# Edge lists on 128 partitions of 416 columns in a four-layer graph network

## The chip, the cores and the metric

The program runs on one core of a Trainium2 chip. The metric is device time in microseconds of one execution. A core has a matrix engine (PE, with its weight loads shown as PEld), a vector engine (DVE, VectorE), a scalar engine (ACT), a general engine (POOL, GpSimd) and a queue engine (SP, SyncE), each of which works through its own list of instructions in order. Data come and go by DMA. In this kernel SP and ACT issue plain transfers, and POOL issues the indirect ones: a gather reads one table row per partition by an index, and a scatter writes one.

## What is computed

The graph has 3125 nodes of 256 features and 53125 directed edges, sorted by destination (`dst`). Every edge has a source (`src`), 64 features (`edge_attr`) and one of 64 types. Four layers follow each other, each on the layer-normed, rectified nodes and each added to them:

```python
h = relu(layernorm(x)); x = x + L0(h)   # messages by an MLP, summed over dst; node MLP; layer norm
h = relu(layernorm(x)); x = x + L1(h)   # attention with a term by edge type, softmax over dst
h = relu(layernorm(x)); x = x + L2(h)   # attention with a term by edge features, softmax over ALL edges
h = relu(layernorm(x)); x = x + L3(h)   # graph attention, softmax over dst, then one LSTM step
```

L2 differs from the others: it takes the softmax over all edges, swaps the two ends of the edge, and therefore wants the edges by their source.

```python
dst, src = edge_index[0], edge_index[1]        # L2 is called with edge_index = (src, dst)
alpha = softmax((q[dst] * (k[src] + edge_attr @ We)).sum(-1) / sqrt(32), axis=0)
out = segment_sum(v[src] * alpha, dst)
```

## The kernel before

**Prelude** (`prelude`, L243). It sorts the nodes by degree and builds all lists. The edge lists are laid out as 125 partitions of 425 columns (`EP, EC`), which holds exactly 53125 edges. `dst_i` is loaded on SP's queue (L254), `e_src`, `e_typ` and `nxt_i`, the destination of the next edge, on ACT's (L261 to L267). `counted` (L325) counts edges per node: VectorE writes one comparison per value (`ol`, `oh`, L330 and L332) over a half of the columns, and PE adds up one outer product per column (L334). `table` (L353) makes the first layer's source rows, which SP stores (L366). The nodes are scattered in sorted order, and for every node the list of its edges' sources and types is gathered from `s_src_type` (`st`).

For L2 every edge gets a place in a table by source, `s_src_records` (`ss`): 440 tiles of 128 rows of 66 numbers (64 features, destination, source within its block of 128 nodes), 18 tiles for each block of 128 source nodes and 8 for the last. VectorE ranks the edges within their block (comparisons L456, running sums L463, then L519 to L555), which ends in the row number `row2`. More rows exist than edges; the whole table is filled beforehand with zeros and a source of -1 by 40 transfers from `sfill` (L305).

**Layers** (`by_slots`, L560). L0 works on 226 pairs of slots. For each, POOL gathers two tiles of source rows (`gt`, L154), PE multiplies edge features (L924), and VectorE adds and sums (L938, L943). L1 goes by blocks of 128 nodes in groups of four slots: per group SP loads the types (`tb`, L980), POOL gathers up to four tiles (`kv`), VectorE forms the scores (L992 to L996), and PE sums the weighted values (L1032). A ring of ten `kv` buffers lies between POOL and these sums. L2 reads `s_src_records` in tiles (`srec`, L1188) and L3 gathers again (`xg`).

**The records are scattered during L0 and L1.** `scatter_src` (L597) scatters one column of edges per call, 425 calls: one per pair from the 19th on, one per step while L0's last work drains, and the rest spread over L1's groups. Columns come in chunks of `CH = 5`: `loaded` (L585) has SP load the features of a chunk into one of two `rec` buffers (L588), and `filled` (L591) has VectorE copy the destination and source into them (L592, L593). Both must wait until the chunk two back has been scattered out of that buffer.

**Order.** Instructions are written in the order of the Python code, and a scheduler places them in each engine's list ahead of what they do not depend on. POOL's gathers and scatters are tied in a written order: `Kit.queued` (L139) sets each scatter after the gather before it and each gather after the last of either kind. An engine waits in order: a load on SP that waits for its buffer holds every transfer behind it.

Of the kernel before, what the change touches and what calls it, by code (L numbers as in the profile page):

```python
# [50 lines left out]
assert sum(TILES) == NT  # L51
XH = 516
# [171 lines left out]
class Lists:  # L224


    def __init__(self, pool):
        self.nid_i = pool.tile([P, NB], I32, name="nid_i")
        self.nid3_i = pool.tile([P, NB], I32, name="nid3_i")
        self.off_i = pool.tile([P, NB], I32, name="off_i")  # L230
        self.deg = pool.tile([P, NB], F32, name="deg")
        self.has = pool.tile([P, NB], F32, name="has")
        self.st = pool.tile([P, NB, SM, 2], I32, name="st")
        self.pen = pool.tile([P, NB, SM], F32, name="pen")
        self.srcb = pool.tile([P, NB, 2, HM], I32, name="srcb")
        self.ai = pool.tile([P, 2, NB], I32, name="ai")
        self.row2 = pool.tile([EP, EC], I32, name="row2")
        self.dst_e = pool.tile([EP, EC], F32, name="dst_e")
        self.srcl_e = pool.tile([EP, EC], F32, name="srcl_e")
# [3 lines left out]
def prelude(ctx, tc, a, a_d, nodes_d, ss, st_d, flag, t):  # L243
# [9 lines left out]
    dst_i = c.tile([EP, EC], I32, name="dst_i")  # L253
    nc.sync.dma_start(dst_i, a["dst"].rearrange("(p c) -> p c", c=EC))  # L254
# [5 lines left out]
    e_src = c.tile([EP, EC], I32, name="e_src")  # L260
    nc.scalar.dma_start(e_src, a["src"].rearrange("(p c) -> p c", c=EC))  # L261
    e_typ = c.tile([EP, EC], I32, name="e_typ")
    nc.scalar.dma_start(e_typ, a["edge_type_64"].rearrange("(p c) -> p c", c=EC))
    nxt_i = c.tile([EP, EC], I32, name="nxt_i")
    nc.gpsimd.memset(nxt_i, N)
    for p0, p1, w in ((0, EP - 1, EC), (EP - 1, EP, EC - 1)):
        nc.scalar.dma_start(nxt_i[p0:p1, 0:w],  # L267
                            bass.AP(tensor=a["dst"].tensor, offset=a["dst"].offset + p0 * EC + 1,
                                    ap=[[EC, p1 - p0], [1, w]]))
# [6 lines left out]
    sfill = c.tile([P, 11, SREC], F32, name="sfill")  # L276
# [12 lines left out]
    nc.gpsimd.memset(cap[:, NB - 1:NB], float(P * TILES[NB - 1]))  # L289
    none = c.tile([1, 512], F32, name="none")  # L290
# [13 lines left out]
    for i in range(40):  # L304
        nc.sync.dma_start(ss[i * 11 * P:(i + 1) * 11 * P, :].rearrange("(p r) c -> p (r c)", p=P),  # L305
                          sfill.rearrange("p r c -> p (r c)"))

    both_e = c.tile([EP, EC, 2], I32, name="both_e")
    nc.gpsimd.tensor_copy(both_e[:, :, 0], e_src)
    nc.gpsimd.tensor_copy(both_e[:, :, 1], e_typ)  # L310
    nc.scalar.dma_start(st_d.rearrange("(p c) -> p c", c=2 * EC), both_e.rearrange("p c i -> p (c i)"))


    lo_i = wk.tile([EP, EC], I32, name="lo_i", tag="edge", bufs=4)
    nc.vector.tensor_scalar(lo_i, dst_i, 127, None, op0=ALU.bitwise_and)
    lo = c.tile([EP, EC], BF, name="lo")
    nc.vector.tensor_copy(lo, lo_i)
    hi_i = wk.tile([EP, EC], I32, name="hi_i", tag="edge", bufs=4)
    nc.vector.tensor_scalar(hi_i, dst_i, 7, None, op0=ALU.logical_shift_right)
    hi = c.tile([EP, EC], BF, name="hi")  # L320
    nc.vector.tensor_copy(hi, hi_i)
    pdeg = ps.tile([P, NB], F32, name="pdeg")
    CW = 214

    def counted(hp, c0, c1):  # L325
        w = c1 - c0
        ol = hp.tile([EP, P, CW], BF, name="ol")
        oh = hp.tile([EP, NB, CW], BF, name="oh")
        for v in range(P):
            nc.vector.tensor_scalar(ol[:, v, 0:w], lo[:, c0:c1], float(v), None, op0=ALU.is_equal)  # L330
        for v in range(NB):
            nc.vector.tensor_scalar(oh[:, v, 0:w], hi[:, c0:c1], float(v), None, op0=ALU.is_equal)  # L332
        for i in range(w):
            nc.tensor.matmul(pdeg, ol[:, :, i], oh[:, :, i], start=(c0 + i == 0), stop=(c0 + i == EC - 1))  # L334
# [33 lines left out]
    with tc.tile_pool(name="ph", bufs=1) as hp:  # L368
        counted(hp, 0, CW)
        stats()  # L370
        table(0, 5)
        counted(hp, CW, EC)
# [73 lines left out]
    sl_i = wk.tile([EP, EC], I32, name="sl_i", tag="edge", bufs=4)  # L446
    nc.vector.tensor_scalar(sl_i, e_src, 127, None, op0=ALU.bitwise_and)
    nc.vector.tensor_copy(t.srcl_e, sl_i)
    hs_i = wk.tile([EP, EC], I32, name="hs_i", tag="edge", bufs=4)
    nc.vector.tensor_scalar(hs_i, e_src, 7, None, op0=ALU.logical_shift_right)  # L450
    hs = c.tile([EP, EC], BF, name="hs")
    nc.vector.tensor_copy(hs, hs_i)
    eq = op.tile([EP, NB, EC], BF, name="eq")
# [3 lines left out]
    zero = ps.tile([EP, EC], F32, name="zero")  # L457
    nc.vector.memset(zero, 0.0)
    cum = op.tile([EP, NB, EC], F32, name="cum")
# [8 lines left out]
    tots = c.tile([EP, NB], F32, name="tots")  # L468
    nc.vector.tensor_copy(tots, cum[:, :, EC - 1])
    pc3 = ps.tile([P, 4, NB], F32, name="pc3")  # L470
    pc2, pv = pc3[:, 0:2, :], pc3[0:1, 2, :]
    nc.tensor.matmul(pc2[:EP, 0, :], k.tri[:EP, :EP], tots, start=True, stop=True)
    nc.tensor.matmul(pc2[:, 1, :], k.ones[:EP, :], tots, start=True, stop=True)
    viol = wk.tile([EP, EC], F32, name="viol", tag="edge", bufs=4)
    nc.vector.tensor_tensor(viol, dst_i, nxt_i, ALU.is_gt)
    v1 = c.tile([EP, 1], F32, name="v1")
# [5 lines left out]
    nc.vector.tensor_tensor(over, pc2[:, 1, :], cap, ALU.is_gt)  # L482
    v3 = c.tile([P, 1], F32, name="v3")
    nc.vector.tensor_reduce(v3, over, AX.X, ALU.add)
    nc.tensor.matmul(pv[:, 0:1], v1, k.ones[:EP, 0:1], start=True, stop=False)
# [5 lines left out]
    bases = c.tile([EP, NB], F32, name="bases")  # L491
    nc.vector.tensor_scalar(bases, pc2[:EP, 0, :], -1.0, None, op0=ALU.add)
# [4 lines left out]
    for b in range(NB - 1, -1, -1):  # L497
        k.gather(t.st[:, b, 0:SLOTS[b], :].rearrange("p s i -> p (s i)"), flat(st_d, 2 * E), t.off_i[:, b:b + 1], axis=1)
# [46 lines left out]
    pos_i = wk.tile([EP, EC], I32, name="pos_i", tag="edge", bufs=4)  # L545
    nc.vector.tensor_copy(pos_i, cum[:, 0])
    pa_i = wk.tile([EP, EC], I32, name="pa_i", tag="edge", bufs=4)
    nc.vector.tensor_scalar(pa_i, pos_i, 127, None, op0=ALU.bitwise_and)
    pj_i = wk.tile([EP, EC], I32, name="pj_i", tag="edge", bufs=4)
    nc.vector.tensor_scalar(pj_i, pos_i, 7, None, op0=ALU.logical_shift_right)  # L550
    step = wk.tile([EP, EC], F32, name="step", tag="edge", bufs=4)
# [3 lines left out]
    nc.vector.scalar_tensor_tensor(t.row2, hs, float(P * TM), step, op0=ALU.mult, op1=ALU.add)  # L555
    nc.vector.tensor_scalar(t.dst_e, dst_i, float(KVQ), None, op0=ALU.mult)
# [3 lines left out]
def by_slots(ctx, tc, a, out, a_d, nodes_d, ss, t):  # L560
# [19 lines left out]
    attr = a["edge_attr_64"].rearrange("(p c) k -> p c k", c=EC)  # L580
    CH = 5
    recs = ctx.enter_context(tc.tile_pool(name="s_recs", bufs=2))
    done = [0]

    def loaded(c):  # L585

        rec = recs.tile([EP, CH, SREC], F32, name="rec")
        nc.sync.dma_start(rec[:, :, 0:64], attr[:, c:c + CH, :])  # L588
        return rec

    def filled(c, rec):  # L591
        nc.vector.tensor_copy(rec[:, :, 64], dst_e[:, c:c + CH])  # L592
        nc.vector.tensor_copy(rec[:, :, 65], srcl_e[:, c:c + CH])  # L593

    rec_of = {}

    def scatter_src(n):  # L597

        for _ in range(n):
            c = done[0]  # L600
            if c == EC:
                return
            c0 = c - c % CH
            if c == 0:
                rec_of[0] = loaded(0)
                filled(0, rec_of[0])
            if c % CH == 1 and c0 + CH < EC:
                rec_of[c0 + CH] = loaded(c0 + CH)
            if c % CH == 3 and c0 + CH < EC:
                filled(c0 + CH, rec_of[c0 + CH])  # L610
            k.scatter(ss, row2[:, c:c + 1], rec_of[c0][:, c % CH, :], "src_records")
# [341 lines left out]
    with tc.tile_pool(name="s_e1", bufs=2) as wk, tc.tile_pool(name="s_e1w", bufs=1) as w, \  # L953
# [159 lines left out]
        left, shares, share = EC - 8 - done[0], sum(-(-c // U) for c in SLOTS), 0  # L1113
# [16 lines left out]
        scatter_src(EC)  # L1130
# [1206 lines left out]
def kernel(tc: tile.TileContext, a: dict, out: bass.AP):  # L2337
# [3 lines left out]
    ss = nc.dram_tensor("s_src_records", [NT * P, SREC], F32, kind="Internal").ap()  # L2341
    st_d = nc.dram_tensor("s_src_type", [2 * E], I32, kind="Internal").ap()
# [43 lines left out]
```

## Time and profile before

| what | before |
|---|---|
| median of 4 runs | 3778.4 us (3776.03 to 3781.05) |
| the profiled execution's own time | 3780.2 us |
| its span | 3778.1 us |
| busy: PE, DVE, ACT, POOL | 2353.4, 2378.4, 1096.8, 2483.7 us |
| mean granted TensorE clock | 0.773 of full |
| moved by DMA | 595.89 MB, mean 158 GB/s |

The span is the time from the first instruction to the last in one profiled execution. The stages can be told apart in the trace: the prelude ends at about 240 us, L0's pairs run from there to 1257 us, what is left of L0 drains until 1387, L1 runs to 2317, L2 to about 3095, and L3 to the end. A line of a group gives the source line, engine, operation, names of output and inputs with their shapes and the count; then busy time and mean nanoseconds of one; then how long the engine stood idle just before, and what ended most of that. Busy time leaves out the short gap between two instructions of an engine. A wait is named by its releaser; "issue" means that nothing in the profile was waited for.

### The profile page before, as it was taken

What the parts mean: (1) busy time and instruction counts of PE and PEld (TensorE: products, weight loads), DVE (VectorE), ACT (ScalarE), POOL (GpSimd) and SP (SyncE); (2) the same over time, 40 slices, a digit from 0 to 9 for tenths busy, and PEclk for the clock granted to TensorE, in tenths of its full rate; (3) what the DMA queues carried; (4) which work ended last, traced back from release to release, by engine and by line L of the source; (5) the groups of instructions that cost most, each with busy time, mean ns of one, the idle gap of its engine ahead of it and who ended that gap; (6) DMA issues with size and microseconds to landing.
All of it is one profiled execution on the core that took longest, in us unless ns stands there. A gap on an engine that the chain in (4) does not pass through costs nothing. (4 is left out here: it accounts for less than half of the span.)

```text
span 3778.1 us, 32562 instructions
## 1 busy us (share of the span) xinstructions
PE 2353.4 (62%) x9174; PEld 1477.7 (39%) x9174; DVE 2378.4 (63%) x4836; ACT 1096.8 (29%) x2296; POOL 2483.7 (66%) x2497
## 2 busy tenths in 40 slices
PE   5818778788877654556656665898989950112223
PEld 3404434344343334445544543566666640001111
DVE  5547566566666426667767765788888953444444
ACT  1112222222221112122322221566666630112222
POOL 3447677777777736767767654666666617667774
PEclk9858989998898765666767767899999975555556
DMA  6336565666666345656666554666666623333342
GB/s 225 128 112 177 138 182 163 171 173 171 183 169 173 84 134 164 173 162 191 188 172 193 170 156 157 204 196 206 198 209 200 192 92 107 100 97 105 108 112 72
DMA packets 295839, 595.89 MB, mean 158 GB/s; under 512 B 113501, under 2 KB 154508, under 8 KB 295650
## 3 DMA queue, kind: packets, MB, share of 16 engines
q0 software_dynamic: 163616, 472.86, 43.2%
q1 hardware_dynamic: 131512, 119.79, 10.6%
q8 instruction: 76, 1.25, 0.1%
q10 hardware_dynamic: 522, 1.06, 0.1%
q14 instruction: 113, 0.93, 0.1%
HBM read 510.85 MB, written 82.21 MB: 157 GB/s over the span
## 5 line engine op out<-in xcount | busy, mean ns | idle before, releaser
L154 POOL DMA_INDIRECT kv<-s_l_rows,dst x440 | 456.1, 1037 | 218.8 <-issue 74.6
L158 POOL DMA_INDIRECT s_src_records<-rec,row x425 | 512.7, 1206 | 131.4 <-issue 121.2
L924 PE MATMUL ph<-wm,st 128*128 128x512 f32 x904 | 473.7, 652 | 131.1 <-DVE acc L943 64.7
L154 POOL DMA_INDIRECT gt<-s_l_src,srcb x452 | 433.8, 960 | 175.9 <-issue 106.1
L154 POOL DMA_INDIRECT kv<-s_l_kv,st x439 | 420.1, 957 | 182.9 <-issue 112.9
L154 POOL DMA_INDIRECT xg<-s_l_rows,src x439 | 416.5, 949 | 133.7 <-issue 133.4
L990 PE MATMUL pk<-rel,toh 64*128 64x64 f32 x878 | 181.8, 368 | 307.8 <-DVE mk L992 180.9
L938 DVE TENSOR_TENSOR ph<-gt,ph 128x1024 f32<-128x1024 f32 x226 | 276.7, 1225 | 109.7 <-PE ph L924 98.3
L134 PE MATMUL pt<-ident,hb 128*128 128x128 f32 x50 | 16.9, 441 | 511.3 <-ACT hb L1436 511.3
L924 PEld LDWEIGHTS ph<-wm,st 128*128 128x128 f32 x904 | 177.7, 207 | 334.4 <-issue 292.8
L990 PEld LDWEIGHTS pk<-rel,toh 64*128 64x128 f32 x878 | 162.5, 272 | 340.9 <-issue 241.2
L1032 PE MATMUL acc<-kv,ident 128*128 128x256 f32 x878 | 246.9, 450 | 40.1 <-DVE kv L1028 40.1
L1287 PE MATMUL pg<-kv,oh 128*128 128x256 f32 x880 | 253.5, 414 | 3.7 <-DVE kv L1284 3.4
L592 DVE COPY rec<-dst_e 125x5 f32<-125x5 f32 x85 | 16.6, 196 | 378.7 <-DMA s_src_records<-rec,row 338.6
L985 ACT ACTIVATE toh<-tb,negp 64x512 f32<-64x512 f32 (+3 forms) x119 | 81.8, 688 | 577.8 <-PE pk L990 510.3
L943 DVE SCALAR_TENSOR_TENSOR acc<-ph,acc 128x1024 f32<-128x1024 f32 x201 | 244.7, 1217 | 3.0
L1032 PEld LDWEIGHTS acc<-kv,ident 128*128 128x128 f32 x878 | 200.1, 231 | 79.9 <-DVE kv L1028 43.5
L1472 DVE TENSOR_SCALAR sc<-xg,own 128x4 f32<-128x4 f32 (+3 forms) x119 | 29.6, 248 | 311.4 <-DMA xg<-s_l_rows,src 311.3
L134 PEld LDWEIGHTS pt<-ident,hb 128*128 128x128 f32 x50 | 7.2, 201 | 540.8 <-ACT hb L1436 540.1
L1429 DVE SCALAR_TENSOR_TENSOR acc<-xg,sc,acc 128x256 f32<-128x256 f32 x439 | 210.5, 487 | 5.2
L1242 PE MATMUL pk<-we,eat 64*128 64x256 f32 x880 | 162.1, 442 | 47.3 <-DVE mk L1248 46.1
L1248 DVE TENSOR_TENSOR mk<-kv,pk 128x512 f32<-128x512 f32 x220 | 149.2, 678 | 48.6 <-DMA kv<-s_l_rows,dst 41.3
(373 smaller groups left out, 5386.7 us busy)
## 6 DMA issues: line engine op xcount, KB each, us to landing
s_src_records<-sfill SPq DMA_DIRECT2D x40, 363.0 KB
srec<-s_src_records SPq DMA_DIRECT2D x24, 594.0 KB
rec<-in_edge_attr_dram SPq DMA_DIRECT2D x85, 156.2 KB
tb<-s_slot_types SPq DMA_DIRECT2D x101, 128.0 KB
gt<-s_l_src,srcb POOLq DMA_INDIRECT x452, 3.6
kv<-s_l_rows,dst POOLq DMA_INDIRECT x440, 3.8
kv<-s_l_kv,st POOLq DMA_INDIRECT x439, 3.9
xg<-s_l_rows,src POOLq DMA_INDIRECT x439, 2.8
```

Of the source, the lines that this page charges most:

```text
L154: self.queued(lambda: self.nc.gpsimd.indirect_dma_start(out=to, out_offset=None, in_=table, in_offset=bass.IndirectOffsetOnAxis(ap=index, ...
L158: st = self.queued(lambda: self.nc.gpsimd.indirect_dma_start(out=table, out_offset=bass.IndirectOffsetOnAxis(ap=index, axis=0), in_=rows, ...
L924: nc.tensor.matmul(ph[:, h, :], stat[h][:, s % 4, :], ms[b][h], start=True, stop=True)
L938: nc.vector.tensor_add(ph, gt, ph)
L943: nc.vector.scalar_tensor_tensor(accs[b], ph, 0.0, accs[b], op0=ALU.max, op1=ALU.add)
L985: nc.scalar.activation(to, tb[:, 0:n * P], AF.Abs, bias=negp[:64])
L990: nc.tensor.matmul(pk[:, q, :], toh[:, q, :], rel, start=True, stop=True)
L1032: nc.tensor.matmul(acc, ident, v[:, q, :], start=(s0 + q == 0), stop=(s0 + q == C - 1))
L1242: nc.tensor.matmul(pk[:, i, :], eat[i * 64:(i + 1) * 64, q, :], we[i * 64:(i + 1) * 64, :], start=True, stop=True)
L1248: nc.vector.tensor_add(mk, o.kv[j // 2][:, :, 0:D], pk)
L1287: nc.tensor.matmul(pg, oh[:, j % T6 + i, :], v[:, i, :], start=(j + i == 0), stop=(j + i == n - 1))
L1429: nc.vector.scalar_tensor_tensor(acc, xgs[q // U3][:, q % U3, 0:D], s[:, q:q + 1], acc, op0=ALU.mult, op1=ALU.add)
```

## The change

The edge lists are laid out on all 128 partitions in 416 columns (`ECW`). Partition 127 then holds 293 edges (`EL`) and 123 places without one. Such a place gets source and destination 4096 and type 0, by transfers of its own from a row of constants, and its record goes to rows that are added behind the table (`past`). Each of the four loads of the prelude is thus made of a part of 127 partitions and small parts for the last one.

The fill of `s_src_records` covers only the last three rows that a partition has in each block (`FULL` counts those that are sure to be overwritten, and a new check, `low`, sends any input with too few edges in a block to the kernel's other path).

The chunk becomes four columns, in a ring of three buffers that are cleared once. The features of a chunk are asked for two chunks ahead instead of one; the copies stay one chunk ahead. A chunk in columns past 293 loads 127 partitions.

All other operations on the edge lists keep their form, with 128 partitions and 416 columns in place of 125 and 425.

```diff
-    dst_i = c.tile([EP, EC], I32, name="dst_i")
-    nc.sync.dma_start(dst_i, a["dst"].rearrange("(p c) -> p c", c=EC))
+    none_i = c.tile([1, 3, ECW], I32, name="none_i")
+    for i, v in enumerate((32 * P, 0, 64 * P)):
+        nc.gpsimd.memset(none_i[:, i, :], v)
+
+    def edges(engine, to, of, i):
+        engine.dma_start(to[0:P - 1, :], of[0:(P - 1) * ECW].rearrange("(p c) -> p c", c=ECW))
+        engine.dma_start(to[P - 1:P, 0:EL], of[(P - 1) * ECW:E].rearrange("(p c) -> p c", p=1))
+        engine.dma_start(to[P - 1:P, EL:ECW], none_i[:, i, EL:ECW])
+
+    dst_i = c.tile([P, ECW], I32, name="dst_i")
+    edges(nc.sync, dst_i, a["dst"], 0)
...
-    e_src = c.tile([EP, EC], I32, name="e_src")
-    nc.scalar.dma_start(e_src, a["src"].rearrange("(p c) -> p c", c=EC))
+    e_src = c.tile([P, ECW], I32, name="e_src")
+    edges(nc.scalar, e_src, a["src"], 0)
...
-    for p0, p1, w in ((0, EP - 1, EC), (EP - 1, EP, EC - 1)):
+    nc.scalar.dma_start(nxt_i[P - 1:P, EL - 1:ECW], none_i[:, 2, EL - 1:ECW])
+    for p0, p1, w in ((0, P - 1, ECW), (P - 1, P, EL - 1)):
...
+    past = c.tile([1, ECW - EL], I32, name="past")
+    nc.gpsimd.iota(past, pattern=[[1, ECW - EL]], base=NT * P, channel_multiplier=0)
+    sfill = c.tile([P, 3, SREC], F32, name="sfill")
...
-    for i in range(40):
-        nc.sync.dma_start(ss[i * 11 * P:(i + 1) * 11 * P, :].rearrange("(p r) c -> p (r c)", p=P),
-                          sfill.rearrange("p r c -> p (r c)"))
+    for b0, b1_ in ((0, 12), (12, NB - 1), (NB - 1, NB)):
+        n = TILES[b0]
+        r0 = b0 * P * TM
+        nc.sync.dma_start(ss[r0:r0 + (b1_ - b0) * P * n, :].rearrange("(b p j) c -> p b (j c)", p=P, j=n)
+                          [:, :, FULL[b0] * SREC:n * SREC],
+                          sfill.rearrange("p r c -> p (r c)")[:, None, :].to_broadcast([P, b1_ - b0, 3 * SREC]))
...
+    nc.vector.tensor_tensor(low, low, pc2[:, 1, :], ALU.is_gt)
+    nc.vector.tensor_add(over, over, low)
...
     nc.vector.scalar_tensor_tensor(t.row2, hs, float(P * TM), step, op0=ALU.mult, op1=ALU.add)
+    nc.sync.dma_start(t.row2[P - 1:P, EL:ECW], past)
...
-    CH = 5
-    recs = ctx.enter_context(tc.tile_pool(name="s_recs", bufs=2))
+    attr = a["edge_attr_64"]
+    CH = 4
+    recs = ctx.enter_context(tc.tile_pool(name="s_recs", bufs=1))
+    ring_ = [recs.tile([P, CH, SREC], F32, name=f"rec{i}") for i in range(3)]
+    for rec in ring_:
+        nc.gpsimd.memset(rec, 0.0)
...
-        rec = recs.tile([EP, CH, SREC], F32, name="rec")
-        nc.sync.dma_start(rec[:, :, 0:64], attr[:, c:c + CH, :])
-        return rec
+        rec = ring_[c // CH % 3]
+        full = min(CH, max(0, EL - c))
+        for p, w0, w1 in ((P, 0, full), (P - 1, full, CH)):
+            if w1 > w0:
+                nc.sync.dma_start(rec[0:p, w0:w1, 0:64],
+                                  bass.AP(tensor=attr.tensor, offset=attr.offset + (c + w0) * 64,
+                                          ap=[[ECW * 64, p], [64, w1 - w0], [1, 64]]))
...
             if c == 0:
-                rec_of[0] = loaded(0)
-                filled(0, rec_of[0])
-            if c % CH == 1 and c0 + CH < EC:
-                rec_of[c0 + CH] = loaded(c0 + CH)
-            if c % CH == 3 and c0 + CH < EC:
-                filled(c0 + CH, rec_of[c0 + CH])
-            k.scatter(ss, row2[:, c:c + 1], rec_of[c0][:, c % CH, :], "src_records")
+                loaded(0)
+                filled(0)
+                loaded(CH)
+            if c % CH == 1 and c0 + 2 * CH < ECW:
+                loaded(c0 + 2 * CH)
+            if c % CH == 3 and c0 + CH < ECW:
+                filled(c0 + CH)
+            k.scatter(ss, row2[:, c:c + 1], ring_[c // CH % 3][:, c % CH, :], "src_records")
```

## The prediction

> **What bounds the kernel now.** I read the page first, for the engines and the costliest groups; then the busy time by stretch, cut where the stages change; then the timeline of POOL; then the waits, and the DMA queues in narrow windows.
>
> ```profile
> PE 2353.4 (62%) x9174; PEld 1477.7 (39%) x9174; DVE 2378.4 (63%) x4836; ACT 1096.8 (29%) x2296; POOL 2483.7 (66%) x2497
> L158 POOL DMA_INDIRECT s_src_records<-rec,row x425 | 512.7, 1206 | 131.4 <-issue 121.2
> L592 DVE COPY rec<-dst_e 125x5 f32<-125x5 f32 x85 | 16.6, 196 | 378.7 <-DMA s_src_records<-rec,row 338.6
> ```
>
> No engine is near full over the span. The scatter of edge records is POOL's costliest group, and VectorE stands idle 338.6 us before the record copies. Both are averages, so I cut the span: L0's pairs (320 to 1257 us), L0's tail, and L1 (1387 to 2317).
>
> ```profile
> core 0: us, PE busy (x) PEld busy (x) DVE busy (x) ACT busy (x) POOL busy (x), PEclk, DMA share, GB/s
> 320.00:1257.00 937.00, 755.10 (x2196) 378.77 (x2195) 590.37 (x850) 197.09 (x401) 708.61 (x682) 0.90 0.59 168
> 1257.00:1337.00 80.00, 41.40 (x94) 21.88 (x92) 23.71 (x66) 7.15 (x15) 63.69 (x54) 0.71 0.28 66
> 1387.00:2317.00 930.00, 542.47 (x2106) 426.68 (x2106) 639.17 (x1035) 217.83 (x357) 639.10 (x624) 0.68 0.62 176
> ```
>
> The same stretches, the scatter of records alone:
>
> ```profile
> 320.00:1257.00 937.00, 252.08 (x208) 0.90 0.59 168
> 1257.00:1337.00 80.00, 61.72 (x52) 0.71 0.28 66
> 1387.00:2317.00 930.00, 198.90 (x165) 0.68 0.62 176
> ```
>
> POOL's timeline shows what its busy figure leaves out, 0.30 us between any two instructions:
>
> ```profile
> 1327.28 0.98 POOL L158 DMA_INDIRECT s_l_kv<-kv,nid_i  x1 [0.30 <-issue]
> 1328.57 1.19 POOL L158 DMA_INDIRECT s_src_records<-rec,row  x1 [0.30 <-issue]
> 1330.06 1.18 POOL L158 DMA_INDIRECT s_src_records<-rec,row  x1 [0.30 <-issue]
> ```
>
> With it POOL is occupied 708.6 + 682 x 0.30 = 913 of 937 us in L0 (97%), all of the tail, and 639.1 + 624 x 0.30 = 826 of 930 us in L1 (89%). POOL bounds L0 and nearly L1, so VectorE's wait at the record copies is mostly VectorE being early.
>
> **The change, part by part.** The profiled execution took 3780.2 us (span 3778.1), 1.8 above the median of 3778.4; I sum against 3780.2 and take 1.8 off at the end.
>
> *The scatter's price.* 425 scatters of 125 rows become 416 of 128. Whatever their row length, the trace's 128-row scatters are cheaper (min/median/max ns):
>
> ```profile
> L158 POOL DMA_INDIRECT s_src_records<-rec,row x425: 1172/1210/1499, 320.3 to 2306.8; - x142
> L158 POOL DMA_INDIRECT s_l_kv<-kv,nid_i x25: 958/998/1011, 505.5 to 1383.5; - x25
> L158 POOL DMA_INDIRECT s_nodes<-xh,rank_i x25: 956/960/4620, 133.7 to 167.7; - x25
> ```
>
> In the timeline above both kinds stand side by side, 0.98 against 1.18. No 128-row scatter of 264-byte rows is in the trace: bounds 0.96 and 1.21. I take 0.98, because the neighbouring rows are nearest in all but row length.
> - L0's pairs: 208 x (1.212 - 0.98) = 48.3; at 97%, **-47**. PE is next: 755 of 890 us, 85%.
> - Tail: 52 x (1.187 - 0.98) = **-11**. Then come 50 us of PE, ACT and VectorE chain with POOL waiting for kv, left as they are.
> - L1: the schedule puts 260 scatters ahead of L1 in both programs, so the nine dropped ones are L1's: 9 x 1.505 = 13.5. The other 156 x (1.205 - 0.98) = 35.1. At 89% of 48.6, **-43**.
>
> *The record loads.* 85 loads of 125 x 5 become 104 chunks of 128 x 4, in a ring of three instead of two. A load waits for the same scatter as before but is needed eight scatters later, not five; a copy waits for a scatter eight back. What a late copy would hold is VectorE's queue, and in L0 POOL is the bound, so I cost this at 0 there; with that cover gone it could give part of the waits named in rival 1. From column 293 on partition 127 holds no edge: 31 loads, all in L1, and one of three columns take 127 partitions. In the tail, one load of now:
>
> ```profile
> DMA packets 692, 0.21 MB, mean 76 GB/s; under 512 B 678, under 2 KB 678, under 8 KB 692
> q1 hardware_dynamic: 617, 0.16, 25.5%
> ```
>
> This window is 1262.05 to 1264.75: 617 of a load's 625 packets of 256 bytes took 0.255 x 16 x 2.7 = 11.0 us of engine time in 2.7 us, 17.9 ns each, so about five engines at once. 125 is 5 x 25; 127 has no divisor, so I take all 508 packets on one engine: 508 x 17.9 = 9.1 us, stretched by the gathers' 0.62 share of it to 9.1 / 0.38 = 24 us at worst. A chunk of four scatters now lasts 930 / 165 x 4 = 22.5 us in L1, and a load has eight scatters of lead, so it should land in time. The transfers for slot types queue behind it on SP, but in the trace they are issued 30 us or more before their use nearly throughout. What is left is the gathers' share on that engine:
>
> ```profile
> DVE mk L992 <- DMA kv<-s_l_kv,st: 53.1, 21, 5.8
> POOL kv L154 <- PE acc L1032: 53.5, 23, 13.8
> ```
>
> I let the first wait grow by a fifth, **+10**; bounds 0 (127 spreads as 125 does) and +112 (rival 2).
>
> *The start.* dst, src, type and next-dst now load 127 partitions each; 25 rows per engine become 127 on one by the same reasoning.
>
> ```profile
> DVE lo_i L315 <- DMA dst_i<-in_dst_dram: 6.7, 1, 6.7
> PE pa L361 <- DMA b<-in_L_gnn_eb_dram: 25.6, 1, 25.6
> q10 hardware_dynamic: 392, 0.64, 7.7%
> ```
>
> The last line is ACT's queue over the first 30 us: 0.077 x 480 / 392 = 94 ns for a packet of some 1.7 KB. dst alone: (127 - 25) x 94 ns = +9.6 us; taking turns with ACT's three loads, +19. VectorE starts later by that, and x and bias b, queued behind dst on SP, hold the first count. Bounds +10 and +22; I take **+16**, since the loads do start together. The small pieces for the last partition, among them the padding behind POOL's three new memsets, are inside the bounds.
>
> *Edits that I cost at little.* The fill shrinks from 40 transfers of 363 KB to three, 2.5 MB in all. SP was through with them at 72 us, when the first row block (70.5 + 0.6) was ready, and from 66.6 to 100.7 PE is busy 34.07 of 34.1 us, which hides it: 0; without that cover the ready row block gains 1 us. PE has 9 count matmuls fewer, 0.7 us. The 2% narrower counts, scans and sums on VectorE give 53 us x 9 / 425 = 1.1. Against these, SP waits for row2 (239.3 us) to patch the padding rows before it reads the flag and loads L0's weights, where it went on at 237.6: with the issue, some 2.5. Three memsets of the ring (0.31 each, by xh's) stand ahead of POOL's first gather: 1. The check's two VectorE instructions (0.2 each) lie beside POOL's slot gathers: 0. Together **+2**.
>
> Sum: -47 - 11 - 43 + 10 + 16 + 2 = -73; 3780.2 - 73 - 1.8 = **3705**.
>
> *The skill against this change.* The trace's row is the load above, about five engines at 125 partitions. The Trainium skill, page "DMA: Bandwidth & Descriptors", section "Why a DMA increments its semaphore by 16 and not by 1", says that a transfer runs on the largest number of engines, at most 16, that divides the slowest dimension of both its sides: 5 for 125, 16 for 128, one for 127. By that rule the loads at the start and in late L1 get slower while the scatters spread; it would give the sum above. By the measured five engines kept for 127, the two terms would go: 3679.
>
> **The rivals.**
> 1. *The deeper ring frees VectorE as well.* For: in L1 POOL waits 53.5 us for PE's acc, which follows VectorE, and VectorE waits 107.8 us there for the scatters. Against: the fills keep POOL's pace in any ring. If 40 of those go and the load term is 0: 3705 - 40 - 10 = 3655.
> 2. *The one-engine loads become L1's bound; slower.* The engine does 0.62 x 22.5 = 14.0 us per chunk besides; it decides once a load costs it over 22.5 - 14.0 = 8.5 us, and with 17.9 ns it costs 9.1. For: that is the edge. Against: the share counts packets waiting for memory. At 24 ns, 12.2 us: 3.6 us x 31 chunks = +112 in place of -43 + 10: 3705 + 33 + 112 = 3850.
> 3. *The same, only to the edge:* L1 gains nothing: 3705 + 33 = 3738, up to 3760 with a slow start.
> 4. *The scatter's price belongs to its short rows* and stays 1.21: only nine calls go, -12: 3778.4 - 12 + 28 = 3794. Against: the 0.98 beside 1.18 above.
>
> **How the numbers follow.** My case 0.58 (its own range 3680 to 3740); rival 1 0.16; rival 3 0.13; rival 2 0.07; rival 4 0.06. A measurement here tells about 0.2%, 7.6 us. Faster: my case, rival 1 and nearly all of rival 3, 0.85; same 0.03; slower, rivals 2 and 4, 0.12. The range leaves out rivals 2 and 4 and a part of rival 1: 3645 to 3775.
>
> **What would show it.** Right: records scatters near 0.98 us; L0's pairs about 47 us shorter; the first VectorE compare after 18 us; L1 30 to 45 us shorter. Wrong: scatters at 1.2 us; POOL waiting for rec's load in L1; gathers landing far later than their median of 3.9 us.

## The result and the profile after

| | before | after |
|---|---|---|
| median | 3777.1 us (62 runs, 3762.4 to 3792.2) | 3787.9 us (38 runs, 3773.9 to 3797.5) |
| after over before | | 1.0027, 95% interval 1.0021 to 1.0033 |
| span of the profiled execution | 3778.1 us | 3786.6 us |

The change makes the kernel slower, by 0.27%. I had forecast 3705 us, 1.9% faster. Since a total can hide gains and losses that meet, the first step is to cut both spans at the same events. Each boundary is the start of a POOL instruction in the trace (us):

| stage | before | after | step | predicted |
|---|---|---|---|---|
| start of the span to the first gather of L0 (`gt`) | 245.7 | 276.6 | +30.9 | +18 (start and handover) |
| to the first record scatter | 74.6 | 74.2 | -0.4 | 0 |
| L0's pairs, to the last `gt` gather | 934.1 | 895.3 | -38.8 | -47 |
| L0's tail, to the first `kv` gather of L1 | 132.9 | 127.6 | -5.3 | -11 |
| L1, to the last scatter of L2's rows | 953.6 | 966.3 | +12.7 | -33 (-43 and +10) |
| L2 and L3 | 1437.2 | 1446.5 | +9.3 | 0 |

The scatters did what was forecast. The page of the kernel after (busy time, mean ns of one, idle before):

```profile
PE 2341.0 (62%) x9165; PEld 1472.2 (39%) x9165; DVE 2375.2 (63%) x4876; ACT 1097.1 (29%) x2296; POOL 2388.7 (63%) x2496
...
L162 POOL DMA_INDIRECT s_src_records<-rec,row x416 | 416.3, 1001 | 128.7 <-issue 118.2
```

A record scatter takes 1001 ns instead of 1206, and POOL is busy 95 us less in the whole program. By stretch (L0's pairs, its tail, L1), the kernel after:

```profile
core 0: us, PE busy (x) PEld busy (x) DVE busy (x) ACT busy (x) POOL busy (x), PEclk, DMA share, GB/s
350.80:1246.10 895.30, 746.94 (x2195) 376.71 (x2194) 590.47 (x870) 197.97 (x401) 667.99 (x681) 0.91 0.61 175
1246.10:1373.70 127.60, 71.96 (x193) 40.40 (x191) 40.69 (x128) 15.12 (x35) 57.31 (x59) 0.70 0.23 66
1373.70:2340.10 966.40, 561.50 (x2158) 436.12 (x2158) 647.33 (x1068) 222.53 (x370) 602.95 (x620) 0.68 0.58 170
```

The scatters alone in the same stretches:

```profile
350.80:1246.10 895.30, 208.76 (x207) 0.91 0.61 175
1246.10:1373.70 127.60, 51.46 (x53) 0.70 0.23 66
1373.70:2340.10 966.40, 156.06 (x156) 0.68 0.58 170
```

In L0 a scatter took 208.76 / 207 = 1.009 us, and the stretch became shorter by nearly what POOL saved. In L1 the 156 scatters took 156.06 us where 165 had taken 198.90, and yet L1 became longer. So there the saving went into another wait. The waits in L1 of the kernel after, over 930 us from its first gather (who waited for what: total us, times, longest):

```profile
ACT toh L1017 <- DMA tb<-s_slot_types: 134.8, 21, 16.9
DVE rec L625 <- DMA s_src_records<-rec,row: 70.4, 13, 9.4
POOL kv L158 <- PE acc L1064: 65.0, 24, 20.2
...
DVE mk L1024 <- DMA kv<-s_l_kv,st: 62.6, 24, 6.8
DVE yg L1100 <- DMA xw<-s_x: 41.9, 4, 12.2
```

The same two waits before, over 930 us from its first gather:

```profile
ACT toh L985 <- DMA tb<-s_slot_types: 67.3, 10, 21.3
...
DVE yg L1068 <- DMA xw<-s_x: 10.1, 3, 5.2
```

ACT's wait for `tb` has doubled, and VectorE's for `xw` has grown fourfold. Both are transfers on SP's queue, and SP's timeline shows what happens to them when a record load of 127 partitions (L619) stands ahead:

```profile
1886.12 0.26 SPq L619 DMA_DIRECT2D rec<-in_edge_attr_dram  x1
1886.48 8.71 SPq L1012 DMA_DIRECT2D tb<-s_slot_types  x1
1895.24 0.58 SPq L1036 DMA_DIRECT2D vb<-s_l_v  x1
```

Issuing the load takes 0.26 us. Issuing the next transfer, `tb`, takes 8.71 us, and everything further down SP's list waits that long too. ACT feels it:

```profile
1899.81 0.72 ACT L1017 ACTIVATE toh<-tb,negp 64x512 f32<-64x512 f32 x1 [11.69 <-DMA tb<-s_slot_types]
```

Over L1, the transfer behind a record load took SP 8.2 us to issue (median of 36; before 1.2), and 29 issues of over 2 us add up to 233.5 us; before there were two, of 4.4 us together. The trace's packets show what goes on meanwhile. The 508 packets of a 127-partition load come one after another for 10.9 us from first to last (median over L1), where the 625 packets of a load before took 3.0. That the next issue waits while such a load drains fits these figures; what inside the queue makes it wait, no view shows.

The start has the same signature. DMA activity of the kernel after in 40 slices of 1 us, first the busy share of the 16 engines in tenths, then GB/s:

```profile
DMA  0000000000259600000018950000000001499995
GB/s 0 0 17 13 25 27 25 33 25 25 89 159 391 199 25 25 25 25 25 27 43 220 385 189 25 24 32 24 26 24 24 25 25 27 64 341 345 343 335 178
```

In 24 of the first 35 slices the whole DMA system moves 13 to 33 GB/s, mostly 25, at a busy share below a tenth. A packet of these loads (1.66 KB) takes 69 ns (median), and 25 GB/s are 15 of them in a microsecond: 15 x 69 ns keep just one engine busy. (The kernel before moves over 100 GB/s in each slice from the fourth to the 28th.) SP gets its list out late:

```profile
1.97 7.40 SPq L265 DMA_DIRECT2D dst_i<-none_i  x1
9.42 24.38 SPq L271 DMA_DIRECT2D xh<-in_x_dram  x4
33.92 0.36 SPq L273 DMA_DIRECT2D xh<-in_x_dram  x1
34.32 7.84 SPq L92 DMA_DIRECT2D w1a<-in_L_gnn_eW_dram  x1
42.20 0.66 SPq L98 DMA_DIRECT2D b<-in_L_gnn_eb_dram  x1
```

The same list before:

```profile
1.20 11.98 SPq L257 DMA_DIRECT2D xh<-in_x_dram  x4
...
18.39 0.73 SPq L94 DMA_DIRECT2D b<-in_L_gnn_eb_dram  x1
```

The bias `b` was issued at 18.39 us before and is issued at 42.20 now. The waits that answer to it in the kernel after:

```profile
PE pa L383 <- DMA b<-in_L_gnn_eb_dram: 52.2, 1, 52.2
...
DVE lo_i L337 <- DMA dst_i<-none_i: 19.8, 1, 19.8
```

PE's wait for `b` stood at 25.6 us before. It has grown by 26.6 us, and POOL enters `by_slots` 26.8 us later (266.3 against 239.5).

### The profile page after: what moved, and what is told of

Its sections match the earlier page's. It is cut to its first block, busy times and chain, and to the rows that moved or that the text cites. A ratio compares the mean times of both kernels' runs of the same rounds, so it can differ in the third digit from the quotient of the medians.

```text
span 3786.6 us, 32564 instructions
## 1 busy us (share of the span) xinstructions
PE 2341.0 (62%) x9165; PEld 1472.2 (39%) x9165; DVE 2375.2 (63%) x4876; ACT 1097.1 (29%) x2296; POOL 2388.7 (63%) x2496
## 5 line engine op out<-in xcount | busy, mean ns | idle before, releaser
L162 POOL DMA_INDIRECT s_src_records<-rec,row x416 | 416.3, 1001 | 128.7 <-issue 118.2
L1064 PE MATMUL acc<-kv,ident 128*128 128x256 f32 x878 | 244.8, 447 | 58.7 <-DVE kv L1060 58.7
L625 DVE COPY rec<-dst_e 128x4 f32<-128x4 f32 x104 | 19.2, 185 | 310.4 <-DMA s_src_records<-rec,row 297.7
L1280 DVE TENSOR_TENSOR mk<-kv,pk 128x512 f32<-128x512 f32 x220 | 149.4, 679 | 51.2 <-DMA kv<-s_l_rows,dst 38.8
```

Of the source, the lines that this page charges most:

```text
L162: st = self.queued(lambda: self.nc.gpsimd.indirect_dma_start(out=table, out_offset=bass.IndirectOffsetOnAxis(ap=index, axis=0), in_=rows, ...
L1064: nc.tensor.matmul(acc, ident, v[:, q, :], start=(s0 + q == 0), stop=(s0 + q == C - 1))
L1280: nc.vector.tensor_add(mk, o.kv[j // 2][:, :, 0:D], pk)
```

## The experiments

Theory A: a transfer over 127 partitions runs on one DMA engine, and this cost the start some 27 us and ate L1's gain. Theory B, for the start: the new memsets and small transfers did it. Theory C, for L1: VectorE and PE set the pace there, and a cheaper scatter was never worth anything. Theory D, for L1: VectorE's copies into `rec` and POOL's wait for `kv` buffers hold each other up, and a deeper ring would free both.

The runs came from five chips. On three of them the kernel before itself took 4193 to 4249 us, so every ratio below is to the kernel before on the same chip in the same set, and stages are compared only between kernels of like total time.

### Cutting the one-engine loads

The edit writes each 127-partition load as two, of 112 and 15 partitions. At the start:

```diff
-        engine.dma_start(to[0:P - 1, :], of[0:(P - 1) * ECW].rearrange("(p c) -> p c", c=ECW))
+        for p0, p1 in ((0, 112), (112, P - 1)):
+            engine.dma_start(to[p0:p1, :], of[p0 * ECW:p1 * ECW].rearrange("(p c) -> p c", c=ECW))
...
-    for p0, p1, w in ((0, P - 1, ECW), (P - 1, P, EL - 1)):
+    for p0, p1, w in ((0, 112, ECW), (112, P - 1, ECW), (P - 1, P, EL - 1)):
```

and for the records:

```diff
-        for p, w0, w1 in ((P, 0, full), (P - 1, full, CH)):
+        for p0, p1, w0, w1 in ((0, P, 0, full), (0, 112, full, CH), (112, P - 1, full, CH)):
             if w1 > w0:
-                nc.sync.dma_start(rec[0:p, w0:w1, 0:64],
-                                  bass.AP(tensor=attr.tensor, offset=attr.offset + (c + w0) * 64,
-                                          ap=[[ECW * 64, p], [64, w1 - w0], [1, 64]]))
+                nc.sync.dma_start(rec[p0:p1, w0:w1, 0:64],
+                                  bass.AP(tensor=attr.tensor, offset=attr.offset + (p0 * ECW + c + w0) * 64,
+                                          ap=[[ECW * 64, p1 - p0], [64, w1 - w0], [1, 64]]))
```

**Both cuts.**

> The changed kernel with all its 127-partition loads cut into 112 and 15 partitions, set against the profile of the changed kernel (3786.6 us span). Theory A: the first gather of L0 25 to 32 us earlier, L1 30 to 45 us shorter, the time about 3725. Rival C (L1's pace is set by VectorE and PE through the kv buffers, and the cheaper scatter is worth nothing there): the start as in A, L1 within 10 us of the changed kernel's 966, the time about 3758, some 20 us under the kernel before.

Measured 3701.6 us, 0.9812 of before (0.9794 to 0.9831). The first gather of L0 comes at 244.8 us, 31.8 earlier than in the kernel after, and L1 takes 918.0 us, 48.3 less. Theory A holds in both places, and the gain is larger than it was put at (the time about 3725, L1 30 to 45 us shorter); theory C would have left L1 where it was. Its DMA activity over the first 40 us, in slices of 1 us, has no such stretch: from the sixth slice to the 27th it moves 177 to 373 GB/s.

```profile
GB/s 0 37 293 97 9 188 332 369 323 350 348 291 346 347 361 373 370 324 317 316 316 252 252 183 229 242 177 59 17 23 0 16 0 0 0 0 0 236 190 0
```

and L1's waits, same kernel:

```profile
DVE rec L626 <- DMA s_src_records<-rec,row: 74.5, 12, 10.1
DVE mk L1025 <- DMA kv<-s_l_kv,st: 48.4, 19, 5.2
...
POOL kv L158 <- PE acc L1065: 40.8, 23, 20.1
ACT toh L1018 <- DMA tb<-s_slot_types: 29.9, 9, 6.6
```

ACT's wait for `tb` is 29.9 us instead of 134.8. A record load now takes 1.8 us from first packet to last, and the transfer behind it 0.45 us to issue. This kernel is faster than the one after, and than the one before on the same chip.

**L1 alone.**

> The changed kernel with only L1's record loads cut. If start and L1 add up: first gather of L0 at 276 us, L1 918 us, the time 48 us under the changed kernel's, about 3738 to 3742.

Measured 3741.8 us, 0.9910 (0.9893 to 0.9926): first gather at 281.9, L1 914.7 us. It is 46 us under the kernel after, its L1 51.6 us shorter, and the start keeps its loss. The start alone with a deeper ring (below) gave 3758.5. So the two nearly add up: 30 and 46 make 76 of the 86 us that both cuts gave.

**The same edits on chips where before took longer.**

> The changed kernel with the four 127-partition loads of the start (dst, src, type, next dst) each cut in two, partitions 0 to 111 and 112 to 126. Theory A (a load of 127 partitions runs on one DMA engine, and that made the start 26.8 us longer): the first VectorE compare, at 21.3 us in the changed kernel against 8.3 before, comes back to 8 to 11 us, POOL reaches the first gather of L0 20 to 27 us earlier than in the changed kernel (276.6 there, 245.7 before), and the time falls by as much, to about 3763. Rival B (the new memsets, the four padding transfers and the more numerous issues delay the start): the compare stays at 18 us or later and the time changes by less than 5 us.

> The changed kernel with only the 127-partition record loads (columns 293 on, nearly all in L1) cut into 112 and 15 partitions. Theory A (the loads on one DMA engine hold back the tb, hb and xw transfers behind them on SP's queue, and this ate L1's gain): L1, from the first gather of kv to the last scatter of s_l_rows, becomes 30 to 45 us shorter than the changed kernel's 966 us, ACT's wait for tb falls from 134.8 us back to about 67, VectorE's wait for xw from 41.9 to about 10; the time falls to about 3750. Rival C (L1 was never bound by POOL; VectorE, PE and the kv buffers set its pace, so cheaper scatters were worth nothing there): those waits fall as well, but L1 becomes shorter by less than 10 us.

> Both cuts at once. Theory A: the sum of the two, about 60 us below the changed kernel: 3725. With rival C for L1: only the start's part, about 3760. With rivals B and C together: unchanged at 3788.

Before took 4193 us there. Measured: start alone 1.0142 (1.0090 to 1.0194), L1 alone 1.0154 (1.0114 to 1.0194), both 1.0086 (1.0052 to 1.0121). The start answers as it should: the first compare starts at 4.7 us with the cut, and the first gather comes at 244.6 and 245.3 us with it, at 274.2 without. That settles the start against theory B, since the memsets and small transfers are still there. But L1 takes 1161.1 us with its loads whole and 1171.7 and 1184.2 with them cut: no gain, although SP's long issues go here too (24 of over 2 us, 161.8 us in all, with the loads whole; one, of 2.1 us, with both cuts). So what theory A says of L1 is shown on chips where before takes its usual time, and not on this one. The waits of the kernel with both cuts suggest that something else holds L1 here:

```profile
ACT toh L1018 <- remote: 467.2, 31, 37.6
...
DVE ph L971 <- remote: 134.4, 25, 8.8
```

"remote" is a releaser that the profile can't place. In all, ACT waits 819 us and VectorE 551 us for it. Every run on the three chips where before took longer has such waits, and no other run has one. In L0's pairs POOL is then occupied 668.5 + 681 x 0.30 = 873 of 1030 us, 85% and not 97%, so a cheaper scatter can be worth less there; how much less is not shown, as there is no profile of before from these chips.

> The changed kernel itself, unaltered, as the base for the runs beside it on the same chip: 0.1 to 0.4% above the kernel before, its start (first gather of L0) some 30 us later than before, L0's pairs some 39 us shorter, L1 no shorter.

> The changed kernel with all its 127-partition loads, at the start and in L1, cut into 112 and 15 partitions. Theory A (one DMA engine carries a 127-partition load; this costs the start about 27 us and L1 30 to 45): against the changed kernel the first gather of L0 comes 25 to 32 us earlier and L1 (first kv gather to last s_l_rows scatter) is 30 to 45 us shorter, the time 55 to 75 us less. Rival C (L1's pace is set by VectorE and PE through the kv buffers): the start as in A, L1 within 10 us of the changed kernel's, the time 25 to 35 us less.

> The same with the ring of record buffers six deep instead of three, so that VectorE's copy of dst and src waits for a scatter 20 back and not 8 back. Theory D (L1's two engines hold each other up: VectorE waits at the copies for POOL's scatters, 70 us, while POOL at other times waits for kv buffers that VectorE and PE free, 65 us, and slack of 8 scatters is too little): VectorE's wait for the scatters falls under 20 us in L1, POOL's wait for acc by half, and L1 is 30 us or more shorter than with three buffers. Against it (where VectorE waits at a copy it is only early, and something else is late next): the waits move to the gathers and L1 changes by less than 8 us.

A second such chip (before 4245 us): the kernel after 1.0145 (1.0103 to 1.0186), both cuts 1.0110 (1.0058 to 1.0163), both with the ring of six 1.0071 (1.0039 to 1.0102). The first gather comes 23 and 30 us earlier with the cuts; L1 takes 1190.7, 1200.8 and 1173.6 us.

> The changed kernel with only the start's 127-partition loads cut into 112 and 15. If start and L1 add up: the time some 32 us under the changed kernel's 3788, at about 3756 (0.994 to 0.995 of before), first gather of L0 at 245 us, L1 still some 966 us. If L1 reacts to the earlier start, L1 differs by more than 10 us.

> The changed kernel with only L1's 127-partition record loads cut into 112 and 15. If the parts add up: first gather of L0 still at 276 us, L1 about 918 us, the time some 48 us under the changed kernel, about 3738 (0.989 of before).

On a third (before 4249 us): start alone 1.0105 (1.0064 to 1.0146), L1 alone 1.0139 (1.0097 to 1.0181), first gathers at 245.6 and 280.7, L1 1185.6 and 1190.1. So on these three chips every form of the new layout that was run took longer than before, those with both cuts too. What holds ACT and VectorE there is open; that it comes from outside the program, as the word and one expectation below have it, is not shown.

### Whether VectorE's copies hold L1 back

```diff
-    ring_ = [recs.tile([P, CH, SREC], F32, name=f"rec{i}") for i in range(3)]
+    ring_ = [recs.tile([P, CH, SREC], F32, name=f"rec{i}") for i in range(6)]
```

with `% 3` made `% 6` in the three places that pick a buffer, on top of both cuts.

> All 127-partition loads cut into 112 and 15, ring of six buffers instead of three. Theory D (VectorE's 74.5 us of waiting for scatters at the record copies in L1 and POOL's 40.8 us for acc hold each other up; more slack frees both): the waits at the copies fall under 20 us in L1 and L1 is 20 us or more shorter than with three buffers (918 us), the time about 3675. Against it (VectorE is only early at the copies): L1 within 8 us of 918, the time within 8 us of 3701.

Measured 3709.2 us, 0.9816 (0.9797 to 0.9834), L1 919.0 us against 918.0. What theory D forecast did not come. Its L1 waits:

```profile
DVE rec L626 <- DMA s_src_records<-rec,row: 91.5, 15, 9.7
...
POOL kv L158 <- PE acc L1065: 50.0, 18, 20.3
```

VectorE's wait did not shrink although the scatter that it needs is now 20 back. The trace shows the reason: a copy that waits starts when the scatter that frees its buffer has landed (for column 284 when 264 have, for 288 when 268, for 292 when 272). The scheduler has moved the copies up in VectorE's list. Counted by the scatters that POOL issues ahead of the next gather that VectorE uses, a copy in L1 stood 2 to 11 scatters ahead of its column with three buffers, and 12 to 24 ahead with six. The slack was given back before the program ran.

So the run did not give VectorE the slack that theory D asks for, and it leaves open whether these waits hold L1 back. They hold more than the copy, as the kernel after shows:

```profile
1743.80 0.17 DVE L625 COPY rec<-dst_e 128x4 f32<-128x4 f32 x1 [5.87 <-DMA s_src_records<-rec,row]
1747.89 1.94 PE L1022 MATMUL pk<-rel,toh 64*128 64x64 f32 x8 [6.86 <-DVE rec L626]
```

VectorE stood 5.87 us at the copy with score products behind it in its list, and PE stood 6.86 us behind VectorE. POOL started a gather or scatter every 1.3 us through all of this, which speaks for VectorE being early, as the prediction had it; that none of it comes back later as a wait of POOL is not shown.

### By which way a one-engine load costs L1

Two kernels with the start cut, six buffers, and L1's loads whole: one as in the change, one with those loads on ACT's queue.

```diff
-                nc.sync.dma_start(rec[0:p, w0:w1, 0:64],
+                (nc.scalar if p == P - 1 else nc.sync).dma_start(rec[0:p, w0:w1, 0:64],
```

> Start cut, ring of six, but L1's record loads whole on 127 partitions, on SP's queue. If the one-engine loads cost L1 its 47 us by themselves (their engine is taken for 10.9 us a load, and whatever needs it waits), a deep ring does not help: 40 to 50 us above the run with the cut loads. If they cost it because each load is late for its scatters, six buffers with the same lead of two chunks change little as well, but POOL or VectorE would be seen waiting for the record load.

> As the run before, with those 127-partition loads issued from ACT's queue instead of SP's. Theory Q (the loss is order on SP's queue: the tb, hb and xw transfers behind a load on the same engine wait their turn behind its 508 packets, 90th percentile of tb's landing 13.1 us against 6.7): on another queue they are no longer behind it, ACT's wait for tb falls from some 130 to under 60 us and 30 us or more of the 47 come back. Theory S (the engine is shared: a load on any queue takes its turns from the kv gathers and tb alike): the waits stay and less than 15 us come back.

On SP's queue: 3758.5 us, 0.9948 (0.9929 to 0.9967), L1 965.1 us, 46 more than with cut loads. No engine waits long for a record load. On ACT's queue: 3737.8 us, 0.9892 (0.9873 to 0.9912), L1 943.3 us. So 22 of the 46 us come back, between what theories Q and S expected. The waits of the run on ACT's queue:

```profile
DVE mk L1025 <- DMA kv<-s_l_kv,st: 58.8, 23, 7.8
POOL kv L158 <- PE acc L1065: 58.4, 25, 20.2
ACT toh L1018 <- DMA tb<-s_slot_types: 11.7, 5, 4.3
...
DVE yg L1101 <- DMA xw<-s_x: 4.9, 4, 2.7
```

The waits for `tb` and `xw` are nearly gone (168.8 and 37.4 us on SP's queue), and none of SP's issues in L1 takes over 2 us (30 do with the loads on its queue, 253.9 us in all). That part is shown: it is SP's list standing still. What stays with ACT's queue is 24 us over the cut kernel, beside VectorE's wait for `kv` gathers at 58.8 us against 48.3 and POOL's for `acc` at 58.4 against 50.0. The gathers themselves land later while the loads are whole. The pages of three kernels with six buffers, in order with the loads cut, whole on SP's queue and whole on ACT's (the last number is the median in us from issue to landing, over the 53 to 59 of the 439 gathers whose landing the profile has):

```profile
kv<-s_l_kv,st POOLq DMA_INDIRECT x439, 4.0
kv<-s_l_kv,st POOLq DMA_INDIRECT x439, 4.9
kv<-s_l_kv,st POOLq DMA_INDIRECT x439, 5.2
```

In L0, where no such load runs, the gathers land after 3.7, 3.6 and 3.7 us in the same kernels. So the one-engine loads hold up the gathers of L1 on either queue. That this makes up all of the 24 us is argued, not shown.

### What L1's scatters are worth

The kernel before without its 165 record scatters of L1, their loads and copies; the rows that they would write keep the fill's values:

```diff
-            if c == EC:
+            if c == 260:
                 return
```

> The kernel before with the scatters, loads and copies of edge records left out from column 260 on, L1's 165 (the output differs). At the 89% of my sum L1 would be 220 us shorter than before's 954; if VectorE and PE set its pace, under 80; the ratio of the gain to 248 us is what a microsecond of scatter is worth there.

Measured 3618.0 us in one run, L1 793.1 us: 160.5 less, for 165 x 1.505 = 248 us of POOL's time. That lies between the expectations: POOL and the chain of VectorE and PE share L1's pace. A microsecond of scatter is worth 0.65 us in L1, less than the 0.89 by which POOL was occupied, and as the loads and copies went with the scatters, part of the 0.65 may be theirs. What bounds L1 without them is partly the chain through the `kv` buffers, POOL's wait for which grows from 53.5 us to:

```profile
POOL kv L154 <- PE acc L1032: 82.6, 33, 19.6
```

> The kernel before with the edge-record scatters, their loads and their VectorE copies left out from column 260 on, that is the 165 of L1 (the rows that they would write keep the fill's values, so the output differs). It asks what L1's scatters cost in all. If POOL bounds L1 as I predicted (89% occupied), 165 x 1.505 = 248 us of POOL's time go and L1, 954 us from the first kv gather to the last s_l_rows scatter, becomes 200 us shorter or more. Rival C (VectorE and PE set L1's pace): it becomes shorter by less than 80 us.

> The kernel before with the edge-record scatters, loads and copies left out from column 260 on, the 165 of L1 (the output differs). If POOL bounds L1 at 89%, L1 is 200 us shorter or more than before's 954 us; if VectorE and PE set its pace, under 80 us; between, both share it, and the ratio of the gain to 248 us is what a microsecond less of scatter is worth there.

On the chips with before at 4193 and 4245 us the same kernel took 4020.7 and 4111.4 us, with L1 at 990.5 and 1007.7 us. No profile of before exists there, so L1's gain can't be read; the totals are 173 and 133 us less.

### Whether five engines cost the kernel before anything

The kernel before with each of its 125-partition loads in two, of 112 and 13 (the next-destination load of 124 in 112 and 12); the records' lines:

```diff
-        nc.sync.dma_start(rec[:, :, 0:64], attr[:, c:c + CH, :])
+        for p0, p1 in ((0, 112), (112, EP)):
+            nc.sync.dma_start(rec[p0:p1, :, 0:64], attr[p0:p1, c:c + CH, :])
```

> The kernel before with its 125-partition loads cut into 112 and 13, on a chip whose cores are not held up from outside. If five engines for 125 partitions cost in the same way as one for 127, only less: the first VectorE compare 3 to 5 us earlier (8.3 us in before), ACT's wait for tb in L1 down from 67 us towards 30, the time 10 to 25 us less. If 3.0 us a load is short enough: within 7 us of before.

Measured 3763.6 us, 0.9960 (0.9945 to 0.9976). ACT's wait for `tb` falls from 67.3 to 37.0 us and the first compare comes at 4.6 us instead of 8.3; yet L1 takes 951.7 us against 953.6, and the first gather comes at 248.4 against 245.7. A small gain whose place the stages of one profile don't show.

> The kernel before, with its 125-partition loads (dst, src, type, next dst and the 85 record loads) cut into 112 and 13 partitions and nothing else changed. If five engines for 125 partitions hurt in the same way as one for 127, only less: the first VectorE compare, at 8.3 us, comes 2 to 5 us earlier, ACT's wait for tb in L1 falls from 67 us towards the 30 of the cut version, and the time is 10 to 25 us less. If a load on five engines is already short enough (3.0 us from first to last packet, against 10.9 on one and 1.8 cut), the time stays within 7 us of before.

On the third chip with a longer time: 0.9976 (0.9944 to 1.0008), undecided.

## Why the prediction was wrong

**Scatter's price: right.** 0.98 us was taken, 1.00 measured. L0's pairs gave -38.8 of -47. Of the 8 us that lack, 207 x (1.009 - 0.98) = 6.0 are the scatters themselves, and 452 `gt` gathers whose median rose from 948 to 956 ns make 3.6. Rival 4, the price of short rows, is out.

**L0's tail:** -11 predicted, -5.3 measured; the two kernels with three buffers and cut record loads gave -9.3. All kernels of the new layout on chips of before's usual time gave 124 to 134 us, and two more profiles of the old layout's tail 124 and 129, so the profiles don't show whether the tail gained.

**L1's scatters: the size was off.** -43 predicted; with the loads cut, L1 gave -35.6. I had multiplied by the share of the time that POOL was occupied. The run without L1's scatters gives 0.65 per microsecond, and 0.65 x 48.6 = 31.6. An occupied share is not yet what a saving is worth. The cut kernel differs from before in two more things that L1 may feel: the ring of three, with which VectorE's wait at the copies is 74.5 us where it was 107.8, and shorter loads (1.8 us for 3.0), of which before itself, with its loads cut in two, had 1.9 us of L1. The ring was not run alone.

**L1's one-engine loads: the step that failed.** I took +10; it is 966.3 - 918.0 = +48. That a load takes one engine was right, and 10.9 us a load is close to the 9.1 that I had at least. (The row beside it was misread: 11.0 us of engine time in 2.7 us are four engines on average, not five.) The wait that I did price, VectorE's for the gathers, grew as I had taken it, from 53.1 to 62.6 us. Beyond that I looked only at whether the load is in time (it is). I set the transfers behind it aside with the sentence that they "are issued 30 us or more before their use nearly throughout". That was read from a trace in which most of SP's issues cost 0.3 to 0.5 us, and those behind a record load 1.2. With a one-engine load ahead, the next issue itself takes 8 us, and the lead is eaten: ACT's wait for `tb` grew by 67.5 us, and 22 of the 46 us went when the loads left SP's queue. Before, two such transfers of 4.4 us in all had been over 2 us, so no row of before showed it; but the same figure stood in its start, where SP took 11.98 us to issue four transfers of `x` behind the load of `dst`, and I read that only as a delay of `x`. Rival 2 had the place and the sign right and its mechanism, the shared engine, at most in half: SP's list standing still was 22 of the 46 us, and the gathers' later landing is the only sign of the rest.

**The start: mis-sized beyond its bounds.** +16 predicted, at most +22; it is 26.8 to `by_slots`, 30.9 to the first gather. I counted `dst` alone, 102 more packets at 94 ns, doubled by taking turns. All four loads sit on the same one engine: 4 x 127 packets of 1.66 KB, which took 35.9 us together by the packet records, 15 in a microsecond where nothing else moves. Other transfers need that engine as well: from 25 to 31 us the records show 9 of these packets in each microsecond and 9 of `x`'s of 1 KB, what is left of `x` taking turns with a load. The first compare came at 21.3 us (forecast: after 18), but the path that counted is PE's wait for `b`. With the cut the first gather is at 244.8 us, against 245.7 before, so the loads account for nearly all of it.

The rule of the Trainium skill that was weighed there, page "DMA: Bandwidth & Descriptors", section "Why a DMA increments its semaphore by 16 and not by 1" (the number of engines is the largest, up to 16, that divides the slowest dimension of both sides: one for 127), agrees with the 25 GB/s of the start and with 10.9 us against 1.8. The prediction used it for the count of engines and still priced its consequence too low.

**The small edits:** +2 predicted for the handover and the rest. Between POOL's entry to `by_slots` and the first gather +4.1 (with the cuts +3.1). L2 and L3 were put at 0 and show +9.3; the other profiles of the changed layout on the chips of before's usual time show +3 to +12. The change leaves the code of these stages as it was, and the cause stays open.

**The sum.** With the measured terms: 30.9 - 0.4 - 38.8 - 5.3 + 12.7 + 9.3 = +8.4, the difference of the spans (+8.5 before rounding). With all the one-engine loads cut the kernel takes 3701.6 us: the gain was there, and these loads took it. That this is near the forecast of 3705 is luck: the forecast had 26 us for the loads in it, and put the gains higher than they were.

Rival 1 as priced is out: with the loads cut L1 gave 35.6 us, not 43 and another 40. That the deeper ring gave a part of the 35.6 is not excluded. Rival 3 (L1 gains nothing) came nearest in L1, for another reason than the edge that it named, and the slow start took the total past it.

## What to carry to other kernels

Before a tile's layout is changed, look at every plain transfer that then covers a partition count such as 127; two transfers of 112 and 15 partitions cost about half a microsecond more of issuing for each load and saved 86 us in all here, on a chip of before's usual time. A slow transfer is to be priced by what stands behind it in its queue and by what shares its engine, and not only by when its own data are needed. A saving on an engine that is occupied 89% of a stage is worth what an experiment says (0.65 here), and slack that a scheduler can see may be gone before the program runs.

## What was not expected of the hardware

- Issuing a transfer took 8.2 us (median) where the transfer ahead of it on the same queue had 508 packets on one engine, against 0.45 us where it was spread. On ACT's queue such loads took 0.2 us to issue themselves, and SP's issues were short.
- One DMA engine moved 25 GB/s in packets of 1.66 KB, and a packet of 256 bytes took 18 ns (median).
- On three of five chips the kernel before took 11 to 12% longer. In the kernel with both cuts on one of them, ACT and VectorE waited 819 and 551 us for a releaser that the profile can't place. On another the change itself was run, and cost 1.45% instead of 0.27%.
- A one-engine load held up other transfers on either queue: the `kv` gathers landed after 4.9 and 5.2 us (median) with the loads whole, against 4.0 with them cut.
